# Two-layer attention on one core: eight ScalarE copies make a row tile that one VectorE product made

## The chip, the core and the metric

The kernel runs on one core of a Trainium2 chip. The metric is the device time of one execution in microseconds. Three runs of the kernel before gave 4740.17, 4742.67 and 4742.81 us: median 4742.67. Engine names: PE is TensorE, PEld its weight loads, DVE is VectorE, ACT is ScalarE, POOL is GpSimd, SP is SyncE, which issues most of the DMAs.

## What is computed

The input is a batch of two images with 256 channels of 64 x 64 points, so N = 4096 positions each. Layer 0 is an attention with four heads of width 16 and a gate; the change doesn't touch it. Layer 1, cut to what matters:

```
qkv = einsum('oc,bchw->bohw', w_qkv, x) + b_qkv        # 768 rows
q, k, v = split(qkv.reshape(b, 4, 3*64, N), 3, axis=2)  # four heads, width 64
attn = softmax(einsum('bhdn,bhdm->bhnm', q, k) / 8)
out = einsum('bhnm,bhdm->bhnd', attn, v).reshape(b, c, h, w)
return einsum('oc,bchw->bohw', w_out, out) + b_out + x
```

Note the reshape: the result of a head is laid out as rows of positions with 64 values each, and these rows are then read as channels.

## The kernel before

Layer 0 fills the first 2100 us or so of the span; layer 1 the rest.

Layer 1 is cut into 32 **units**: image b (2), pair of heads g (2), block j of 512 query positions (8). A unit runs over NM = 32 **chunks** of 128 key positions. The chunks form NG = 2 **groups** of GS = 16: each group has its own running maximum, its own sum of exponentials and its own accumulated output, and the two are joined at the end of the unit.

What one chunk costs, with the lines:

- `score` (L861): PE forms the scores of two heads into a PSUM pair of banks, 128 keys x 2 x 512 queries. The pool of pairs has two buffers.
- `keep` (L878, L879): DVE takes the running maximum; ACT copies the scores to SBUF, into a ring of 24 tiles called `raw`.
- `shift` (L944): some 20 chunks later DVE adds the negated maximum.
- `weigh` (L956, L968): ACT takes the exponential in place, POOL adds the tile to the group's sum `acc`. The first add of a group (L966) takes two tiles.
- `gather` (L978): PE multiplies by the values and accumulates `av` in PSUM.

So two streams run together: scores of the present chunk, and shift, exponential and gather of the chunk 20 places before.

At the end of a group: PE transposes the running maximum (`turn_max`, L886), DVE reduces it (`fold`, L898), POOL splits the result into three bf16 parts (`split`, L909 to L912), PE turns these back (`turn`, L925), ACT copies them (L930), PE spreads them (`spread_shift`, L939), and the next shift can start.

At the end of a unit, while the next unit's scores run: PE sums `acc` over the partitions (`total`), ACT copies the sums (L1016) and takes an exponential of 128x8 (L1018), PE transposes them, DVE forms the factors `f` (L1035 to L1038), POOL one more of them (L1039). Then, for the second group and after it for the first, PE transposes the accumulated output (`turn_sums`, L1023, through `turned`), and `rows` multiplies the turned tile by its factors: a 128 x 4 x 2 x 64 tile, where each of the 4 x 2 pieces of 64 has its own factor on every partition (L1049). For the second group POOL adds the bias (L1056), for the first POOL adds the two halves (L1060), and two DMAs on SP write the result out.

All these small PSUM results (the turned tiles, the turned maxima, the products for the queries, keys and values) use one pool with **one** bank, called misc. A product into it can start only when the previous user has been read.

The order on each engine is written out by hand: every instruction is kept in program order, and a table of hooks says in which step and at which place of it ("start", "early", "early end", "late", "late end") an extra piece stands. A step handles a pair of chunks. The hooks for the end of a unit are:

```
at(t1 + 5, "late", lambda u=u: turn_sums(u, 1))
at(t1 + 5, "late end", lambda u=u: rows(u, 1))
at(t1 + 6, "early", lambda u=u: turn_sums(u, 0))
at(t1 + 6, "early end", lambda u=u: rows(u, 0))
```

with `t1 = t0 + US + GS // 2`. Around them stand the score products of the next unit's chunks 28 to 31, and the product for the queries of the unit after it (`next_queries`, L672), which also uses misc and is copied by ACT (`keep_queries`, L699).

Of the kernel before, what the change touches and what calls it, by code (L numbers as in the profile page):

```python
# [10 lines left out]
AF = mybir.ActivationFunctionType  # L11
ALU = mybir.AluOpType
# [3 lines left out]
P = 128  # L16
# [5 lines left out]
D1 = 64  # L22
# [5 lines left out]
def conv_attention_kernel(  # L28
# [19 lines left out]
    nc = tc.nc  # L48
# [3 lines left out]
    PB = NB // P  # L52
# [167 lines left out]
    seq = tc.keep_in_program_order  # L220
# [24 lines left out]
    with own0:  # L245
# [134 lines left out]
        def prep_dyn(four):  # L380

            ps = prep_bank("dynp_{}_{}".format(*four[0]))
            for i, u in enumerate(four):
                seq(nc.tensor.matmul(
                    ps[32 * i : 32 * i + 32, :], c2rep, work.pop(("d1", *u)),
                    start=True, stop=True,
                ))
            rows = prep.tile([P, NB], F32, tag="dyn", bufs=1, name="dynrows_{}_{}".format(*four[0]))
            seq(nc.scalar.activation(rows, ps, AF.Identity, bias=c2b))
            for i, (b, j) in enumerate(four):  # L390
                nc.sync.dma_start(out=dyn0[b][j], in_=rows[32 * i : 32 * i + 1, :])
# [330 lines left out]
        for i in range(NJ):  # L722
            k = (0, 0, i)
# [54 lines left out]
    with (  # L778
# [10 lines left out]
        avs1, srows, losts, joined, halves = {}, {}, {}, {}, {}  # L789
# [255 lines left out]
        def rows(u, n):  # L1045
            b, g, j = u
            ps = avs1.pop((u, n))
            r = l1.tile([P, PB, 2, D1], F32, tag="rows", name=f"rows_{b}_{g}_{j}_{n}")
            seq(nc.vector.tensor_tensor(  # L1049
                r, ps, joined[u][:, n].unsqueeze(3).to_broadcast([P, PB, 2, D1]), ALU.mult  # L1050
            ))
            last = u == units[-1]
            if n == 1:
                halves[u] = r
                bias = b1v[:, 2 * g : 2 * g + 2, :].unsqueeze(1).to_broadcast([P, PB, 2, D1])
                seq(nc.gpsimd.tensor_tensor(r, r, bias, ALU.add))  # L1056
                return
            joined.pop(u)
            engine = nc.vector if last else nc.gpsimd
            seq(engine.tensor_tensor(r, r, halves.pop(u), ALU.add))  # L1060


            if last:
                for k in range(2):
                    c = ((2 * g + k) * N + j * NB) // D1 % P
                    for i in range(PB):
                        (nc.sync if k else nc.scalar).dma_start(
                            out=last_att[0][c + 2 * i : c + 2 * i + 2, :].rearrange(
                                "q (s d) -> q s d", d=D1
                            ),  # L1070
                            in_=r[:, i, k, :],
                        )
                return
            to = att[b].rearrange("(h q) (s d) -> h (q s) d", h=H, d=D1)
            for k in range(2):
                nc.sync.dma_start(
                    out=to[2 * g + k, bass.ts(j, NB), :].rearrange("(i q) d -> q i d", q=P),
                    in_=r[:, :, k, :],
                )
# [29 lines left out]
        for n, u in enumerate(units):  # L1109
# [32 lines left out]
            at(t1 + 5, "early end", lambda u=u: factors(u))  # L1142
# [4 lines that stand above are left out]
            if b < B - 1 and (g, j) == (PR - 1, NJ - 1):  # L1147
                for i in range(NJ):
# [156 lines left out]
```

## Time and profile before

| quantity | value |
|---|---|
| median of three runs | 4742.67 us |
| the profiled execution, its own time | 4741.58 us |
| its span in the profile | 4739.8 us |
| granted TensorE clock | 0.996 |
| L1049 on DVE | 64 instructions, median 686 ns |
| period of an ordinary unit of layer 1 | 81.30 us |
| period of four units that also project the first image out | 88.75 us |
| period of units that prepare no keys and values | 79.19 us |

The period is the distance between the starts of the first L1049 of neighbouring units. A line of the timeline has the start and the length in us, the engine, the line of the code, the operation, output and inputs with their shapes, the number of instructions merged into it, and in brackets the idle time of the engine just before it, with what ended that. In a line of the groups the three fields after the shapes are the busy time in us with the mean in ns, and the idle time before.

### The profile page before, as it was taken

Reading aid. Unit: us, or ns where it says so; the run is one execution under the profiler, and the core shown is the slowest. Engines: PE = TensorE matmul, PEld = TensorE weight load, DVE = VectorE, ACT = ScalarE, POOL = GpSimd, SP = SyncE. Lnnn points to the kernel's source line nnn. Section 1 sums busy time; section 2 is a strip of 40 time slices with the busy share of each in tenths; the row PEclk is TensorE's granted clock in tenths of the full one; section 3 lists DMA queues with packets and bytes.
Section 4 is the critical chain, followed back from the end, with each engine's and each line's share of the span. In section 5 each row is a group of like instructions: output and inputs, shape, how many; then the busy total and the mean of one; then the engine's idle time right before and its main releaser. Section 6 shows DMA issues by size and latency. Waiting matters only on the chain.

```text
span 4739.8 us, 70643 instructions
## 1 busy us (share of the span) xinstructions
PE 4526.9 (96%) x27506; PEld 1496.2 (32%) x27506; DVE 3917.0 (83%) x4584; ACT 3394.1 (72%) x4508; POOL 2540.6 (54%) x1491
## 2 busy tenths in 40 slices
PE   8999999999999999989999999999999999999998
PEld 3433333333333333333232232323233332222222
DVE  6777777777777777359999999999999899999996
ACT  3366666666666666668888888888887778888884
POOL 6300000000000000039999999999998889999994
PEclk9999999999999999999999999999999999999999
DMA  3100000000000000110000100001111111000002
GB/s 103 34 4 19 19 21 15 15 15 15 15 15 15 15 13 13 57 63 25 23 25 17 54 30 23 25 23 36 52 36 45 63 52 47 18 14 7 14 16 74
DMA packets 113381, 140.10 MB, mean 30 GB/s; under 512 B 51864, under 2 KB 52696, under 8 KB 112932
## 3 DMA queue, kind: packets, MB, share of 16 engines
q1 hardware_dynamic: 111260, 135.11, 9.2%
q8 instruction: 216, 3.54, 0.3%
q14 instruction: 121, 0.99, 0.1%
q10 hardware_dynamic: 1784, 0.46, 0.0%
HBM read 93.58 MB, written 41.70 MB: 29 GB/s over the span
## 4 chain that ended last, share of the span: by engine, by line
PE 58%; DVE 15%; POOL 15%; issue 6%; ACT 5%; DMA 1%; SPq 0%; ACTq 0%; DVEq 0%; POOLq 0%
PE s L448 24%; POOL acc L968 13%; PE av L463 12%; DVE rmax L878 10%; PE s L861 6%; PE av L978 5%; DVE raw L944 4%; ACT raw L879 4%; PE a L410 2%; PE p L270 1%; PE k1p L672 1%; POOL acc L966 1%; PE rt L886 1%; PE q1p L672 1%; PE o L549 1%
## 5 line engine op out<-in xcount | busy, mean ns | idle before, releaser
L968 POOL TENSOR_TENSOR acc<-acc,raw 128x1024 f32<-128x1024 f32 x884 | 2098.1, 2373 | 89.4 <-ACT raw L956 30.2
L414 DVE TENSOR_REDUCE mx<-a 128x1 f32<-128x512 f32 x2048 | 1315.3, 686 | 450.5 <-PE a L410 449.4
L451 ACT ACTIVATE p<-s 128x512 f32<-128x512 f32 x2048 | 1109.8, 597 | 701.3 <-PE a L410 367.3
L944 DVE TENSOR_TENSOR raw<-raw,shift 128x1024 f32<-128x1024 f32 x1024 | 1238.0, 1213 | 19.2 <-PE shift L939 12.7
L861 PE MATMUL s<-q,k 64*128 64x512 f32 x4096 | 1117.2, 636 | 142.9 <-ACT raw L879 134.6
L878 DVE TENSOR_TENSOR rmax<-s,rmax 128x1024 f32<-128x1024 f32 x960 | 1170.1, 1219 | 72.7 <-PE s L861 70.8
L879 ACT COPY raw<-s 128x1024 f32<-128x1024 f32 x1024 | 1037.7, 1013 | 259.4 <-DVE rmax L878 173.5
L448 PE MATMUL s<-q,kT 32*128 32x512 f32 x4096 | 1219.1, 640 | 0.0
L956 ACT ACTIVATE raw<-raw 128x1024 f32<-128x1024 f32 x1024 | 1086.9, 1062 | 178.4 <-DVE raw L944 147.3
L410 PE MATMUL a<-kT,q 32*128 32x512 f32 x4096 | 1129.7, 643 | 1.2 <-DVE mx L414 1.0
L978 PE MATMUL av<-raw,v 128*64 128x512 f32 x4096 | 999.3, 606 | 2.0
L463 PE MATMUL av<-p,v 128*32 128x256 f32 (+1 forms) x7904 | 650.2, 399 | 0.6 <-ACT avs L477 0.6
L861 PEld LDWEIGHTS s<-q,k 64*128 64x128 f32 x4096 | 317.1, 185 | 827.9 <-ACT raw L879 628.0
L513 POOL TENSOR_TENSOR f<-f,dyn 128x16 f32<-128x16 f32 x15 | 3.3, 223 | 1028.2 <-DVE f L512 1028.2
L448 PEld LDWEIGHTS s<-q,kT 32*128 32x128 f32 x4096 | 397.9, 183 | 426.3 <-issue 392.1
L978 PEld LDWEIGHTS av<-raw,v 128*64 128x64 f32 x4096 | 243.3, 136 | 587.6 <-issue 428.8
L463 PEld LDWEIGHTS av<-p,v 128*32 128x32 f32 x7904 | 157.6, 108 | 751.5 <-issue 737.3
L564 POOL TENSOR_SCALAR res<-res 128x1024 f32<-128x1024 f32 x16 | 16.8, 1049 | 660.5 <-ACT res L563 660.5
L410 PEld LDWEIGHTS a<-kT,q 32*128 32x128 f32 x4096 | 305.0, 184 | 31.4 <-DVE mx L414 18.2
L966 POOL TENSOR_TENSOR acc<-raw,raw 128x1024 f32<-128x1024 f32 x64 | 152.4, 2381 | 112.7 <-ACT raw L956 103.8
L898 DVE TENSOR_REDUCE negs<-rt 128x4 f32<-128x512 f32 x128 | 88.3, 690 | 50.1 <-PE rt L886 47.6
L318 DVE RECIPROCAL std<-std 128x128 f32<-128x128 f32 x64 | 56.1, 920 | 37.7 <-ACT std L313 37.7
(332 smaller groups left out, 1840.4 us busy)
## 6 DMA issues: line engine op xcount, KB each, us to landing
x<-in_x_dram SPq DMA_DIRECT2D x16, 512.0 KB
res<-in_x_dram SPq DMA_DIRECT2D x16, 512.0 KB
x<-res SPq DMA_DIRECT2D x16, 512.0 KB
att<-rows SPq DMA_DIRECT2D x62, 128.0 KB
kd<-k1s SPq DMA_DIRECT2D x24, 256.0 KB
vd<-v1s SPq DMA_DIRECT2D x24, 256.0 KB
k<-kd SPq DMA_DIRECT2D x24, 256.0 KB
v<-vd SPq DMA_DIRECT2D x24, 256.0 KB
```

Source lines behind the costliest of these rows:

```text
L410: seq(nc.tensor.matmul(ps, qs0[u][r, bass.ts(i, P)], kTs[b][r, bass.ts(m, NB)], start=True, stop=True,))
L414: seq(nc.vector.tensor_reduce(mxs[u][:, i * H + h, m : m + 1], ps, AX.X, ALU.max))
L448: seq(nc.tensor.matmul(ps, kTs[b][r, bass.ts(m, P)], qs0[u][r, :], start=True, stop=True))
L451: seq(nc.scalar.activation(pt[:, k, :], ps, AF.Exp, scale=D0**-0.5))
L463: seq(nc.tensor.matmul(avs[u][32 * h : 32 * h + 32, cols], vs0[b][:, m, 32 * h : 32 * h + 32], pts[t, h // 2][:, h % 2, cols], start=(m == ...
L861: seq(nc.tensor.matmul(ps[:, k, :], ks[b, g, m // PB][r, bass.ts(m % PB, P)], qs1[u][r, :], start=True, stop=True,))
L878: seq(nc.vector.tensor_tensor(rmax[u, n], ps, before, ALU.max))
L879: seq(nc.scalar.copy(raw, ps))
L944: seq(nc.vector.tensor_tensor(raws[t], raws[t], shifts[u, t % NM // GS], ALU.add))
L956: seq(nc.scalar.activation(p, p, AF.Exp, scale=D1**-0.5))
L968: seq(nc.gpsimd.tensor_tensor(accs[u, n], accs[u, n], p, ALU.add))
L978: seq(nc.tensor.matmul(avs1[u, n][k * D1 : (k + 1) * D1, :], v[:, m % PB, k, :], raws[t][:, k, :], start=(m % GS == 0), stop=(m % GS == GS ...
```

## The change

In `rows`, the tile of the second group (n == 1) is made on ScalarE by eight activations, one for each of the 4 x 2 pieces of 64 columns, with the function Copy and the factor as a scale per partition. The tile of the first group stays on VectorE, and so do both tiles of the last unit. The rest is as before: POOL adds the bias to the same tile.

```
             r = l1.tile([P, PB, 2, D1], F32, tag="rows", name=f"rows_{b}_{g}_{j}_{n}")
-            seq(nc.vector.tensor_tensor(
-                r, ps, joined[u][:, n].unsqueeze(3).to_broadcast([P, PB, 2, D1]), ALU.mult
-            ))
             last = u == units[-1]
+            if n == 1 and not last:
+                for i in range(PB):
+                    for k in range(2):
+                        seq(nc.scalar.activation(
+                            r[:, i, k, :], ps[:, i, k, :], AF.Copy,
+                            scale=joined[u][:, n, i, k : k + 1],
+                        ))
+            else:
+                seq(nc.vector.tensor_tensor(
+                    r, ps, joined[u][:, n].unsqueeze(3).to_broadcast([P, PB, 2, D1]), ALU.mult
+                ))
             if n == 1:
```

## The prediction

> **What bounds the kernel now.** I read the engine shares first, then a table of busy time over one unit of layer 1, then the timeline around the changed step, and last the groups for the durations of ScalarE's instructions.
>
> The engine shares say only that no engine can be left out:
> ```profile
> PE 4526.9 (96%) x27506; PEld 1496.2 (32%) x27506; DVE 3917.0 (83%) x4584; ACT 3394.1 (72%) x4508; POOL 2540.6 (54%) x1491
> ```
> In layer 1 the units repeat with a fixed period. One period of it (columns: window, length, then busy time of PE, PEld, DVE, ACT, POOL):
> ```profile
> core 0: us, PE busy (x) PEld busy (x) DVE busy (x) ACT busy (x) POOL busy (x), PEclk, DMA share, GB/s
> 3167.52:3248.82 81.30, 76.69 (x330) 24.33 (x330) 76.35 (x72) 68.51 (x73) 75.52 (x43) 1.00 0.08 23
> ```
> PE 94%, DVE 94%, POOL 93%, ACT 84%: three engines share the bound, so what counts is which wait ends last where the change sits. The start of the first L1049 (call it t) in two units, and the bias add that follows it on POOL:
> ```profile
> 3004.79 0.69 DVE L1049 TENSOR_TENSOR rows<-turned,f 128x512 f32<-128x512 f32 x1
> 3007.45 1.28 POOL L1056 TENSOR_TENSOR rows<-rows,b1v 128x512 f32<-128x512 f32 x1
> 3086.23 0.69 DVE L1049 TENSOR_TENSOR rows<-turned,f 128x512 f32<-128x512 f32 x1 [0.16 <-PE turned L1023]
> 3088.74 1.28 POOL L1056 TENSOR_TENSOR rows<-rows,b1v 128x512 f32<-128x512 f32 x1
> ```
> One period is 81.30 us nearly everywhere (88.75 in the four units that also project the first image out, 79.19 in those that prepare no keys). In the second unit here L1049 comes 0.14 us late (81.44 later) while POOL is on time (81.29 later); the unit after it (t = 3167.52, its L1056 at 3170.18 below) is late by that 0.14 in both. So a delay in this stretch lasts, and POOL doesn't absorb it. Now the stretch itself, at t = 3167.52:
> ```profile
> 3167.41 2.40 PE L861 MATMUL s<-q,k 64*128 64x512 f32 x8
> 3167.52 0.69 DVE L1049 TENSOR_TENSOR rows<-turned,f 128x512 f32<-128x512 f32 x1
> 3167.61 1.01 ACT L879 COPY raw<-s 128x1024 f32<-128x1024 f32 x1 [0.62 <-POOL acc L968]
> 3168.13 1.21 DVE L944 TENSOR_TENSOR raw<-raw,shift 128x1024 f32<-128x1024 f32 x1
> 3169.38 1.06 ACT L956 ACTIVATE raw<-raw 128x1024 f32<-128x1024 f32 x1 [0.75 <-DVE raw L944]
> 3169.74 0.66 PE L1023 MATMUL turned<-ident,avs 128*128 128x128 f32 x4
> 3170.18 1.28 POOL L1056 TENSOR_TENSOR rows<-rows,b1v 128x512 f32<-128x512 f32 x1
> 3170.33 1.94 PE L978 MATMUL av<-raw,v 128*64 128x512 f32 x8
> 3171.52 0.68 DVE L1049 TENSOR_TENSOR rows<-turned,f 128x512 f32<-128x512 f32 x1
> 3172.26 1.12 PE L672 MATMUL q1p<-b_('q', (0, 1, 6))_25737,w 128*128 128x512 f32 x2
> 3174.51 0.30 PEld L861 LDWEIGHTS s<-q,k 64*128 64x128 f32 x4 [0.90 <-ACT raw L879]
> ...
> 3188.26 0.40 PE L925 MATMUL nm1p<-ident,negmax 128*128 128x128 bf16 x4 [0.54 <-POOL negmax L912]
> ...
> 3190.05 1.13 PE L861 MATMUL s<-q,k 64*128 64x512 f32 x4 [0.33 <-ACT raw L879]
> ```
> What to see: PE goes from scores to the second turn (3169.74), gather, and query product without a gap; the second turn starts as the scores end. The turned tile is PSUM's one "misc" bank, so the second turn also needs the first to have been read: today that is done at 3168.21, 1.5 us early. PE's path and DVE's (rows, shift, max, shift, rows to 3172.20) meet at the query product within about 0.06 us. Both are critical; ACT idles 0.75 us in between.
>
> [...]
> ```profile
> L995 ACT COPY avs<-av 128x512 f32<-128x512 f32 x49 | 29.1, 593 | 0.0
> L699 ACT ACTIVATE q<-q1p,b 128x512 f32<-128x512 f32 x25 | 16.8, 672 | 0.0
> L1018 ACT ACTIVATE lost<-lost 128x8 f32<-128x8 f32 x25 | 5.3, 213 | 0.0
> ```
> A pointer adds 672 - 593 = 79 ns, and the start of the next instruction lies about 100 ns before the end in all three. [...] the built instruction list of the changed kernel has the same three table loads as before, so no switch is charged.
>
> **The change, part by part.**
>
> Removed: 31 of the 64 L1049 on DVE (the last unit keeps its own). Each occupies DVE for 0.61 us (3167.52 to 3168.13), 18.9 us in all. It only counts where DVE alone is late.
>
> Added: 31 x 8 = 248 activations of 128x64 from PSUM. From the 1024- and 512-element copies the slope is (1013 - 593) / 512 = 0.82 ns per element, so one lasts 672 - 448 x 0.82 = 305 ns, and one starts every 205 ns. 8 x 0.205 = 1.64 us of ACT per unit, 51 us in all. Bounds: 150 ns (the 110 ns of L1018's start to start plus 46 for 56 more elements, the pointer free) and 300 ns (no overlap).
>
> Order, read off the built list: the eight stand on ACT behind the copy L879 at t + 0.09 and ahead of the exponential L956. No DMA, SP or GpSimd instruction changes place. Only the first waits (for PE's turn, long done). They start at t + 1.00 (the next instruction follows 0.91 after a 1024-element copy) and end at t + 1.00 + 7 x 0.205 + 0.305 = t + 2.74.
>
> Behind them on ACT: the exponential starts at t + 2.64 instead of t + 1.86, ends at 3.70, and the gather that reads it is due on PE at about 4.3, so 0.6 us of slack hides it. The score copies after it: the first is 0.4 us later, with its bank not wanted until t + 5.8; the next comes earlier than now, as DVE is ahead. Cost zero; if the eight took over 300 ns each, this cover would go.
>
> Who waits for the eight: (a) POOL's bias add, at t + 2.66 now, would start at 2.80: 0.14 late. POOL's next stall is on its own input, and PE's wait for POOL at 3188.26 is followed by a 0.33 us wait for ACT at 3190.05, so 0.33 us of this costs nothing. (b) PE's second turn, at t + 2.22 now, must wait for the bank: 2.74 + 0.06 (the gap from an ACT end to the PE start it releases, 3168.62 to 3168.68) = t + 2.80. PE stalls 0.58 us, with everything queued behind in order: gather, query product, scores, the max transposes.
>
> What PE gets back: 0.06 at the query product, and 0.11 at the score at 3174.51 (3173.32 to the next product at 3175.57 is 2.25 us for what elsewhere takes 2.14, waiting for a copy behind DVE, which is now earlier). Net 0.58 - 0.17 = 0.41 us per unit. From there to the second max transpose PE has no gap, and DVE's next reduce waits for it, so it lasts to the next unit.
>
> Sum: 26 ordinary units x 0.41 = 10.7 us. In the four long units the query product waits 0.40 us for DVE's second rows today, and PE's stall of about 0.5 takes its place: 0.05 each, 0.2 in all. In the last of the 31 no query product follows and DVE is the late one: 0.5 back. Total 10.4 us. The profiled execution took 4741.58 us (span 4739.80 and 1.78 around it), 1.09 below the median of 4742.67: 4752.0 against its own time, 4753 against the median.
>
> **The rivals.**
>
> 1. Not slower: POOL's chain sets the period, and PE's slip vanishes in its 0.54 us wait for the split at 3188.26. Then only POOL's 0.14 us stays, 31 x 0.14 = 4.3 us: 4747. Or the eight are quicker than I think: at one per 170 ns they cost 0.13 a unit, 4747. For it: POOL is 93% busy and that wait is real. Against: the unit at 3086.23, whose 0.14 us passed a punctual POOL. It decides if the slip stays below 0.54 and the wait at 3190.05 were not there.
> 2. Much slower: no overlap, or a pointer reload per copy. At one per 250 to 300 ns the slip is 0.77 to 1.07 us a unit instead of 0.41: 31 times that is 24 to 33 us, 4767 to 4776. No row shows eight small pointer activations in a row, so this stays open; L699 among its neighbours speaks against.
> 3. Faster: DVE alone is the bound, and 31 x 0.61 = 18.9 us come back: 4724. The point is the bank: the eight would have to end before t + 2.16, so one per 130 ns, and even then PE's path allows only 0.17 us a unit (4737). DVE's 94% speaks for it, the seamless PE against.
> 4. That the change isn't done as said is excluded by the built list (248 activations in place, 31 DVE rows gone).
>
> **How the numbers follow.** A measurement here tells about 0.2%, 9.5 us, from no change: the limits are 4733 and 4752.2. My forecast, 4749 to 4760, has 0.55, of which 0.45 lies above 4752.2; rival 1 (4742 to 4749) 0.22; rival 2 (from 4760 up) 0.19; rival 3 0.04. Slower 0.45 + 0.19 = 0.64, same 0.10 + 0.22 = 0.32, faster 0.04. The range from 4744 to 4772 leaves out rival 3, the lowest of rival 1 and the upper half of rival 2.
>
> **What would show it.** In the changed profile: the eight at 300 ns each, one every 205; PE idle about 0.58 us before the second turn, released by ACT; DVE's second rows at about t + 3.5 with a wait for PE; the period 81.7 us. Wrong if the period stays at 81.30 with that stall there (rival 1), if the eight take over 2 us together (rival 2), or if the second turn doesn't wait (rival 3).

## The result and the profile after

The changed kernel takes 4755.47 us (median of eight runs, 4754.04 to 4756.58). The kernel before, run beside it, takes 4741.19 (4740.17 to 4742.81). The ratio is 1.0029, 95% interval 1.0018 to 1.004: slower by 0.29%, with an interval from 0.18 to 0.4%. That is 2.5 us above the predicted 4753.0, which was reckoned from the median of 4742.67; set against the kernel before as it ran beside, 14.3 us were added where 10.4 had been forecast. The profiled execution took 4755.49 us, its span is 4753.7 (4739.8 before), the granted clock 0.996 as before: the difference to explain is 13.9 us of span.

Line numbers move with the change: in the profile after, L1053 are the eight activations, L1058 is VectorE's row (L1049 before) and L1064 is POOL's bias add (L1056 before).

The engine shares of the page after, first; they moved as the instruction counts say and do not show a loss:
```profile
PE 4519.8 (95%) x27506; PEld 1498.6 (32%) x27506; DVE 3900.1 (82%) x4553; ACT 3428.2 (72%) x4756; POOL 2538.7 (53%) x1491
```
The table of one ordinary unit shows it (window, length, then the busy time of each engine):
```profile
core 0: us, PE busy (x) PEld busy (x) DVE busy (x) ACT busy (x) POOL busy (x), PEclk, DMA share, GB/s
3174.51:3256.32 81.81, 76.43 (x330) 24.41 (x328) 75.80 (x72) 69.67 (x83) 75.42 (x43) 1.00 0.08 23
```
The period, here from one unit's first L1053 to the next one's, went from 81.30 to 81.81 us. DVE has 0.55 us less to do in it and ACT 1.16 more, and every engine but ACT idles more than before: PE 5.38 us of the unit instead of 4.61. So the added 0.51 us is a wait on PE and not work of PE's.

The timeline of the changed stretch. It answers to the stretch shown of before, and its times are to be set against that one's plus 5.99 us, by which the unit stands later up to here (first L879 of both lists):
```profile
3173.60 1.01 ACT L879 COPY raw<-s 128x1024 f32<-128x1024 f32 x1 [0.62 <-POOL acc L968]
3174.51 1.75 ACT L1053 ACTIVATE rows<-turned,f 128x64 f32<-128x64 f32 x8
3176.09 1.12 ACT L956 ACTIVATE raw<-raw 128x1024 f32<-128x1024 f32 x1
3176.31 0.66 PE L1023 MATMUL turned<-ident,avs 128*128 128x128 f32 x4 [0.52 <-ACT rows L1053]
3176.34 1.28 POOL L1064 TENSOR_TENSOR rows<-rows,b1v 128x512 f32<-128x512 f32 x1 [0.17 <-ACT rows L1053]
3177.06 0.69 DVE L1058 TENSOR_TENSOR rows<-turned,f 128x512 f32<-128x512 f32 x1
3178.77 1.13 PE L672 MATMUL q1p<-b_('q', (0, 1, 6))_25821,w 128*128 128x512 f32 x2
3179.82 1.99 PE L861 MATMUL s<-q,k 64*128 64x512 f32 x8
3181.00 1.23 DVE L878 TENSOR_TENSOR rmax<-s,rmax 128x1024 f32<-128x1024 f32 x1 [0.99 <-PE s L861]
3181.74 1.12 PE L672 MATMUL q1p<-b_('q', (0, 1, 6))_25821,w 128*128 128x512 f32 x2
3185.07 2.03 PE L861 MATMUL s<-q,k 64*128 64x512 f32 x8 [0.34 <-ACT q L699]
3190.18 0.69 DVE L898 TENSOR_REDUCE negs<-rt 128x4 f32<-128x512 f32 x1 [0.64 <-PE rt L886]
3194.39 0.40 PE L925 MATMUL nm1p<-ident,negmax 128*128 128x128 bf16 x4 [0.16 <-POOL negmax L912]
3196.55 1.13 PE L861 MATMUL s<-q,k 64*128 64x512 f32 x4 [0.71 <-ACT raw L879]
```
and the lines of before that are needed beside it and were not shown yet:
```profile
3175.57 1.12 PE L672 MATMUL q1p<-b_('q', (0, 1, 6))_25737,w 128*128 128x512 f32 x2
3178.57 2.03 PE L861 MATMUL s<-q,k 64*128 64x512 f32 x8
3180.53 0.66 PE L886 MATMUL rt<-ident,rmax 128*128 128x128 f32 x4
3183.68 0.69 DVE L898 TENSOR_REDUCE negs<-rt 128x4 f32<-128x512 f32 x1 [0.63 <-PE rt L886]
```
Following the slip, each line's time less its time before and less 5.99: the second turn 0.58 (its own idle time is 0.52), the first half of the query product 0.52, its second half 0.18, the next group of scores 0.51 with a wait of 0.34 for ACT's query copy L699, DVE's reduce 0.51, the shift transpose nm1p only 0.14, the scores after it 0.51. So PE nearly catches up twice (at 3181.74 and at 3194.39) and both times a wait for ACT puts it back.

The view of line L1053, the added instructions: fastest, median and slowest in ns, then who waited for them (us in all, times):
```profile
L1053 ACT ACTIVATE rows<-turned,f x248: 316/336/368, 2192.8 to 4660.3; 128x64 f32<-128x64 f32 x124
  PE turned L1023: 15.9, 31
  POOL rows L1064: 2.8, 7
```
PE waits for them in each of the 31 units, 15.9 us in all: already more than the 13.9 us lost.

### The profile page after: what moved, and what is told of

The parts are those of the page before. It is cut to its first block, busy times and chain, and to the rows that moved or that the text cites. A ratio compares the mean times of both kernels' runs of the same rounds, so it can differ in the third digit from the quotient of the medians.

```text
span 4753.7 us, 70860 instructions
## 1 busy us (share of the span) xinstructions
PE 4519.8 (95%) x27506; PEld 1498.6 (32%) x27506; DVE 3900.1 (82%) x4553; ACT 3428.2 (72%) x4756; POOL 2538.7 (53%) x1491
## 4 chain that ended last, share of the span: by engine, by line
PE 58%; POOL 15%; DVE 13%; ACT 7%; issue 6%; DMA 1%; SPq 0%; ACTq 0%; DVEq 0%; POOLq 0%
PE s L448 24%; POOL acc L968 13%; PE av L463 12%; DVE rmax L878 9%; PE s L861 6%; PE av L978 5%; DVE raw L944 4%; ACT raw L879 3%; ACT raw L956 2%; PE a L410 2%; POOL acc L966 1%; PE p L270 1%; ACT rows L1053 1%; PE rt L886 1%; PE k1p L672 1%
## 5 line engine op out<-in xcount | busy, mean ns | idle before, releaser
L878 DVE TENSOR_TENSOR rmax<-s,rmax 128x1024 f32<-128x1024 f32 x960 | 1169.2, 1218 | 102.9 <-PE s L861 101.7
L879 ACT COPY raw<-s 128x1024 f32<-128x1024 f32 x1024 | 1037.9, 1014 | 262.6 <-DVE rmax L878 175.5
L898 DVE TENSOR_REDUCE negs<-rt 128x4 f32<-128x512 f32 x128 | 88.2, 689 | 50.0 <-PE rt L886 47.5
```

The source lines that it names most:

```text
L878: seq(nc.vector.tensor_tensor(rmax[u, n], ps, before, ALU.max))
L879: seq(nc.scalar.copy(raw, ps))
```

## The experiments

**The theory.** The loss comes from how long the turned tile's one PSUM bank is held: a reader that starts 1.0 us later on ACT and takes 1.75 us keeps PE from its second turn, and the slip travels with the scores. **Rivals.** A: ACT's queue has 1.6 us more in it per unit, and what stands behind (exponential, score copies) comes late, whatever bank it reads. B: DVE is the bound, and only the size of the relief matters. C: POOL's late bias add sets the period.

### Half on each engine

Edit on the changed kernel: VectorE takes the first two of the four blocks in one instruction, ScalarE the other two in four.
```
-                for i in range(PB):
+                seq(nc.vector.tensor_tensor(
+                    r[:, :2], ps[:, :2],
+                    joined[u][:, n, :2].unsqueeze(3).to_broadcast([P, 2, 2, D1]), ALU.mult
+                ))
+                for i in range(2, PB):
```


> VectorE makes the pieces of the first two query blocks of the second group's tile in one instruction, ScalarE the other four pieces. Theory (the bank is held): ScalarE's four end about 1.95 us after the mark t (the time at which the turned tile is ready for the first reader), before the second turn is due at t + 2.22, so TensorE doesn't stall and the time goes back to that of the kernel before: 4739 to 4743 us. Rival A (it is ScalarE's added work in its queue): half of the work leaves half of the loss, about 4748. Rival B (VectorE's work is what bounds the unit): 31 x 0.27 us are gained, about 4733.

Measured: 4738.39 us (4736.67 to 4739.16) beside 4740.99 of the kernel before; ratio 0.9994 (0.9986 to 1.0002). The period is 81.20 us. Its timeline, one unit earlier than in the lists above, as are the later ones with times near 3100 (L1051 is VectorE's half, L1057 ScalarE's four):
```profile
3084.33 0.42 DVE L1051 TENSOR_TENSOR rows<-turned,f 128x256 f32<-128x256 f32 x1
3085.33 0.94 ACT L1057 ACTIVATE rows<-turned,f 128x64 f32<-128x64 f32 x4
3086.54 0.66 PE L1023 MATMUL turned<-ident,avs 128*128 128x128 f32 x4
3095.30 2.03 PE L861 MATMUL s<-q,k 64*128 64x512 f32 x8 [0.19 <-ACT q L699]
```
The four are done at 3086.27, the second turn starts 0.27 us later without a wait, and the whole loss is gone. Half of ACT's added load is still there, so A would have kept about half the loss. The period is 0.10 us shorter than before for 0.27 us less on VectorE, so relief of DVE seems worth something, but less than its size (the interval of the ratio includes 1): B doesn't bound alone.

### ScalarE's load without the bank

Edit on the kernel before: seven activations of the same form at the same place, reading and writing SBUF tiles that nobody waits for.
```
             last = u == units[-1]
+            if n == 1 and not last:
+                spare = l1.tile([P, 7, D1], F32, tag="spare", bufs=1, name=f"spare_{b}_{g}_{j}")
+                for i in range(7):
+                    seq(nc.scalar.activation(
+                        spare[:, i, :], b1v[:, 0, :], AF.Copy,
+                        scale=joined[u][:, n, i // 2, i % 2 : i % 2 + 1],
+                    ))
```


> The kernel before, with seven extra activations of 128x64 on ScalarE at the place where the changed kernel has its eight. They read a constant in SBUF and write a spare tile that nobody reads, so they add work that the result doesn't need. [...] Theory (the bank is held): VectorE still frees the bank early, TensorE's second turn doesn't wait, and the time stays within 3 us of the kernel before: 4741 to 4745. Rival A (ScalarE's added work): the whole loss appears, about 4755.

Measured: 4741.26 us; ratio 1.0001 (0.9993 to 1.0009), period 81.33. Its timeline:
```profile
3167.17 0.69 DVE L1049 TENSOR_TENSOR rows<-turned,f 128x512 f32<-128x512 f32 x1
3168.17 1.79 ACT L1056 ACTIVATE spare<-b1v,f 128x64 f32<-128x64 f32 x7
3169.38 0.66 PE L1023 MATMUL turned<-ident,avs 128*128 128x128 f32 x4
3169.86 1.04 ACT L956 ACTIVATE raw<-raw 128x1024 f32<-128x1024 f32 x1
```
The seven start one per 0.24 us where the eight start one per 0.20, so ACT is occupied for 1.79 us, as long as by the eight, and the exponential comes after them; PE's turn doesn't wait, and nothing is lost. What reaches PE is that the next gather lasts 2.06 us instead of 1.94, and the unit absorbs it. A is out for this place: the same load costs nothing when the bank is left to VectorE.

### The bank held late, without the load

Edit on the kernel before: VectorE makes the tile as before, and one more ScalarE copy of 64 columns of the same bank stands just ahead of the second turn. Its output is unused.
```
+                held[u] = ps
...
+        def peek(u):
+            spare = l1.tile([P, D1], F32, tag="spare", bufs=1, name="spare_{}_{}_{}".format(*u))
+            seq(nc.scalar.copy(spare, held.pop(u)[:, 0, 0, :]))
...
+            if u != units[-1]:
+                at(t1 + 6, "early", lambda u=u: peek(u))
             at(t1 + 6, "early", lambda u=u: turn_sums(u, 0))
```


> The kernel before, with one extra ScalarE copy of 128x64 from the turned tile of the second group, placed behind the exponential that follows; what it writes is not used. It adds only about 0.2 us of ScalarE work per unit but holds the bank until about t + 3.1. Theory (the bank is held): the second turn on TensorE starts at t + 3.15 instead of t + 2.22, 0.06 of that is given back, 0.88 us a unit remain: 31 x 0.88 = 27 us, about 4768. Rival A (ScalarE's added work): an eighth of the loss, about 4743. Rival B (VectorE's relief counts): no change, 4741.

Measured: 4765.04 us; ratio 1.0051 (1.0037 to 1.0065), period 82.06. Its timeline:
```profile
3176.79 0.69 DVE L1049 TENSOR_TENSOR rows<-turned,f 128x512 f32<-128x512 f32 x1
3178.64 1.06 ACT L956 ACTIVATE raw<-raw 128x1024 f32<-128x1024 f32 x1 [0.76 <-DVE raw L944]
3179.42 1.30 POOL L1058 TENSOR_TENSOR rows<-rows,b1v 128x512 f32<-128x512 f32 x1
3179.60 0.19 ACT L1085 COPY spare<-turned 128x64 f32<-128x64 f32 x1
3179.85 0.33 PE L1023 MATMUL turned<-ident,avs 128*128 128x128 f32 x1 [0.78 <-ACT spare L1085]
```
One copy of 190 ns per unit, on an engine that had just idled 0.76 us ahead of its exponential, costs 24.05 us, or 0.76 a unit: what PE waits for the bank, and not what the instruction lasts. POOL's bias add starts 2.63 us after VectorE's row, as in the kernel before (2.66), so it is not late here and C isn't needed for the loss. Together with the run before, this carries the theory from both sides: load without the hold is free, and the hold without the load costs.

### The query copy ahead of the score copy

In the changed kernel PE had recovered to a slip of 0.18 by its second half of the query product, and lost it again by waiting for ACT's query copy. That copy stands on ACT behind a score copy and an exponential that wait for DVE, and DVE's maximum (L878 at 3181.00) had itself waited 0.99 us for the late scores: the slip goes round PE's recovery by way of DVE and ACT. Edit on the changed kernel: a new hook ahead of the exponential's step, and the query copy moved to it.
```
-                at(t0 - 1, "early end", lambda u=u: keep_queries(u))
+                at(t0 - 1, "before weigh", lambda u=u: keep_queries(u))
...
+                hung(t, "before weigh")
```


> The changed kernel, with the copy of the next queries on ScalarE moved ahead of one exponential. In the changed kernel TensorE makes up 0.33 us at the last scores of a unit and loses it again waiting for this copy. Theory (the copy is where the given-back time is lost): the copy ends about 0.95 us earlier, that wait of 0.34 us goes, 26 to 31 units x 0.33 = 9 to 10 us return: about 4746. Rival (the loss is passed on another way, by the chain of maxima and the transposes): no change, 4755.

Measured: 4748.27 us; ratio to the kernel before 1.0015 (1.0008 to 1.0021), so some 7 us of the loss are gone, less than the 9 to 10 expected. The period is 81.63.
```profile
3173.41 0.66 PE L1023 MATMUL turned<-ident,avs 128*128 128x128 f32 x4 [0.52 <-ACT rows L1053]
3179.40 1.01 ACT L879 COPY raw<-s 128x1024 f32<-128x1024 f32 x1 [1.21 <-DVE rmax L878]
3180.31 0.69 ACT L699 ACTIVATE q<-q1p,b 128x512 f32<-128x512 f32 x1
3181.76 2.28 PE L861 MATMUL s<-q,k 64*128 64x512 f32 x8
```
The stall at the turn stays at 0.52, and the wait for the query copy is gone. But the group of scores now lasts 2.28 us instead of 2.03: ACT's score copy ends only inside it, at 3182.85 (1.01 us from 3181.84), and its second half probably waits for that. Of the 0.33 us that PE could have kept, 0.18 a unit is kept.

### Half and half with the moved copy, and the moved copy alone

The first run has both edits; the second has the moved query copy on the kernel before.

> The half-and-half kernel (VectorE makes four pieces of the second group's tile in one instruction, ScalarE the other four), with the copy of the next queries on ScalarE moved ahead of one exponential. In the half-and-half kernel TensorE still waits 0.19 us a unit for that copy, and behind it 0.61 us for GpSimd's split, of which 0.26 is covered by a later wait. Theory (that copy is now what ends last): 26 to 31 units x 0.19 are gained over 4738.4: about 4733. Rival (GpSimd's split sets the unit now): no gain, 4738.

> The kernel before, with only the copy of the next queries on ScalarE moved ahead of one exponential. Theory (in the kernel before VectorE's path holds up the last scores of a unit, so the copy isn't late there): no change, 4739 to 4742. Rival (the copy is late in every version): the gain of 7 us that it brought in the changed kernel comes here too, 4734.

Measured: half and half with the moved copy 4734.53 us (4732.96 to 4735.8), ratio 0.9985 (0.9979 to 0.9992), period 81.06: faster than the kernel before by 0.15%. The moved copy alone 4738.12, ratio 0.9992 (0.9984 to 1.0), period 81.18. The interval of the second reaches 1, but the period of its trace is 0.12 us shorter. So the copy was tied for last in the kernel before as well, which I had not expected: moving it gains 0.12 a unit there, 0.14 on top of the half, 0.18 in the changed kernel. The kernel before, first two lines, and the moved copy alone:
```profile
3176.63 1.94 PE L978 MATMUL av<-raw,v 128*64 128x512 f32 x8
3178.56 0.30 PEld L861 LDWEIGHTS s<-q,k 64*128 64x128 f32 x4 [0.88 <-ACT q L699]
3175.41 1.94 PE L978 MATMUL av<-raw,v 128*64 128x512 f32 x8
3177.28 1.99 PE L861 MATMUL s<-q,k 64*128 64x512 f32 x8
```
From the gather to the scores it takes 1.94 us before (3176.63 to 3178.57) and 1.87 with the moved copy. The list gives PE no idle time in the first; the starts show it, and so does the weight load's wait. The scores then take 1.96 us to the next transpose (3178.57 to 3180.53) and 1.91 with the moved copy, which is the rest of the 0.12. The timeline of half and half with the moved copy:
```profile
3085.78 0.66 PE L1023 MATMUL turned<-ident,avs 128*128 128x128 f32 x4
3094.27 2.14 PE L861 MATMUL s<-q,k 64*128 64x512 f32 x8
```
From the turn to these scores it takes 8.49 us, with no wait in the list between them, where half and half alone takes 8.76 and the changed kernel 8.76 behind its stall.

### The query product elsewhere, and the turn later

If PE alone sets this stretch, then work taken out of it should give its length back, up to the next other limit. Edit on the kernel before: the query product (two halves, 2.1 us of PE) moved four and five steps earlier, with its fetch and its copy.
```
-                at(t0 - 5, "start", lambda u=u, b=b, j=j: fetch(("q", u), x1[b][j]))
-                at(t0 - 2, "late", lambda u=u: next_queries(u, 0))
-                at(t0 - 1, "early", lambda u=u: next_queries(u, 1))
-                at(t0 - 1, "early end", lambda u=u: keep_queries(u))
+                at(t0 - 9, "start", lambda u=u, b=b, j=j: fetch(("q", u), x1[b][j]))
+                at(t0 - 6, "late", lambda u=u: next_queries(u, 0))
+                at(t0 - 6, "late", lambda u=u: next_queries(u, 1))
+                at(t0 - 6, "late end", lambda u=u: keep_queries(u))
```


> The kernel before, with the product for the next queries and its copy moved five steps ahead, out of the stretch in which TensorE has no gap, to the middle of the unit. Theory (that stretch sets the unit): up to 1.0 us a unit leaves the stretch, but GpSimd's split allows only 0.33 of it: about 10 us gained, 4731. Rival (TensorE is as full in the middle of the unit): the 2.1 us come back there, 4741 or above.

The second run makes this edit on the changed kernel and also turns the first group's sums later, behind the gather (`turn_sums(u, 0)` at `(t1 + 6, "late")`, `rows(u, 0)` at `(t1 + 6, "late end")`), so that the eight have time to end.

> The changed kernel, with the query product five steps ahead and, on TensorE, the second turn behind the two gathers that follow it, so that the eight activations have freed the bank when it is due. Theory (the bank is held): TensorE's stall of 0.5 us is gone although ScalarE still makes all eight, and the time is within 4 us of the kernel with only the early query product. Rival A (ScalarE's added work): some 14 us above that kernel.

Both missed. The first took 4764.1 us, ratio 1.0046 (1.0033 to 1.0058), period 82.22, where I had expected a gain. The first two lines are from the product's new place, the others from its old one:
```profile
3079.26 1.98 PE L672 MATMUL q1p<-b_('q', (0, 1, 5))_25130,w 128*128 128x512 f32 x4
3086.99 1.13 PE L861 MATMUL s<-q,k 64*128 64x512 f32 x4 [0.91 <-ACT raw L879]
3098.28 0.66 PE L1023 MATMUL turned<-ident,avs 128*128 128x128 f32 x4
3100.66 1.22 DVE L878 TENSOR_TENSOR rmax<-s,rmax 128x1024 f32<-128x1024 f32 x1
3101.99 1.01 ACT L879 COPY raw<-s 128x1024 f32<-128x1024 f32 x1 [0.75 <-PE s L861]
3103.05 1.13 PE L861 MATMUL s<-q,k 64*128 64x512 f32 x4 [1.19 <-ACT raw L879]
3108.61 0.66 PE L886 MATMUL rt<-ident,rmax 128*128 128x128 f32 x4
```
At the old place the second half of the scores starts 4.77 us after the turn (3098.28 to 3103.05), and in the kernel before, with half of the product still ahead of it, it starts 4.77 us after it too (3169.74 to 3174.51). What sets it in both is the line of DVE's row, DVE's maximum and ACT's score copy; the profile names PE for the copy's wait here, but in program order the copy follows the maximum that ends at 3101.88, and in the kernel before the same copy waits 0.75 us for DVE by name. So PE waits 1.19 us there, and from the turn to the first max transpose only 0.46 us of the 2.1 come back (10.33 us against 10.79). The unit is 0.92 longer all the same, so the new place costs 1.38: the product takes 1.98 us there in one piece, of which an idle time of PE right behind it takes up a part (0.72 in the kernel before, at 3153.95), and a wait for ACT further on is 0.91 where it was 0.45 (3158.45). Why that wait grew was not tried apart.

The second took 4776.25, ratio 1.0072 (1.0059 to 1.0086), period 82.62, 0.40 above the first where I had expected the two to agree:
```profile
3101.60 1.75 ACT L1053 ACTIVATE rows<-turned,f 128x64 f32<-128x64 f32 x8
3104.35 1.08 PE L978 MATMUL av<-raw,v 128*64 128x512 f32 x4 [0.46 <-ACT raw L956]
3105.36 0.65 PE L1023 MATMUL turned<-ident,avs 128*128 128x128 f32 x4
3106.11 0.69 DVE L1058 TENSOR_TENSOR rows<-turned,f 128x512 f32<-128x512 f32 x1 [0.95 <-issue]
3112.48 1.13 PE L861 MATMUL s<-q,k 64*128 64x512 f32 x4 [1.13 <-ACT raw L879]
```
The bank's wait is gone, as intended. In its place the gather, now ahead of the turn, waits 0.46 us for the exponential behind the eight. The 0.6 us of slack that hid the late exponential came from the turn and PE's stall, which both stood ahead of the gather. The turn is later for both reasons, its new place and that wait; DVE's row starts as the turn ends, after 0.95 us of idling, and DVE then has no gap up to the maximum whose score copy PE waits for (1.13 us at 3112.48). So rival A has a point from which it matters: once the gather comes first, ACT's queue is one link of the chain that ends last. How much of the 0.40 is the queue's and how much the later turn's was not tried apart.

## Why the prediction was right, and what was off

**Right: the mechanism and its place.** PE's second turn waits for the eight, in each of the 31 units. The slip of its start is 0.58 in the unit shown, as predicted, and the eight end 2.75 us after the mark t, which is 3173.51 here (2.74 predicted).

**The eight copies.** They last 336 ns at the median and not 305, but start one per 0.20 us against 0.205 (1.75 us from the first start to the last end, less the last one's length, by seven). The prediction took both from the slope of the large copies and the overlap in the trace before; the length was 31 ns short, and the rate, which matters, was right. The profile after shows three table loads of 1.28 us, as the one before does, so the eight added none. Rival 2's rate of 250 to 300 is out. Two of the rivals' sums count eight intervals where only seven lie between the starts: one per 250 ns would make the slip 0.73 and not 0.77, one per 170 ns 0.17 and not 0.13.

**The step that was off: what PE gets back.** I took 0.06 at the query product and 0.11 at the score that waited for a copy behind DVE, 0.17 in all. The first came as said (0.58 to 0.52). The second was larger than thought (0.52 to 0.18): I had set the 2.25 us of that group of scores against 2.14 elsewhere, but 2.14 holds a wait too, and a group without one takes 1.92 (after, 3179.82 to 3181.74). Then almost all of it was lost at the next scores, where PE waits 0.34 for the query copy, a wait that I had put at nothing. What is kept is 0.07, so the slip is 0.51 instead of 0.41. My statement that PE has no gap from there to the second max transpose held only for the idle times that the list gives: by the starts PE already waited 0.07 for that copy in the kernel before, and the moved copy gained 0.12 a unit there. I had looked for slack on PE alone and not on the line that feeds it. That the total came out within 2.5 us of the forecast is therefore in part luck: one give-back was taken too small and its loss was left out.

**How the slip gets past POOL.** Rival 1 was half true: at nm1p PE stands only 0.14 late, since POOL's split sets it, and the wait for POOL fell from 0.54 to 0.16. But the wait for ACT's score copy right after it grew from 0.33 to 0.71, by the same 0.38. The slip doesn't go over PE there but over DVE, as the prediction had it: the reduce L898 waits for PE's max transposes, is 0.51 late, and the score copies follow DVE. POOL's own delay was 0.17 against 0.14, and cost nothing.

**The sum.** The distances between neighbouring units (reciprocal to reciprocal on DVE) add up as follows:

| distances | predicted | measured |
|---|---|---|
| 24 ordinary | 24 x 0.41 = 9.8 | 11.75 (0.51 in nearly all) |
| 5 around the long units | 4 x 0.05 + 0.41 = 0.6 | 1.09 |
| the one before the last | 0.41 | 0.86 |
| the last | -0.5 | -0.42 |
| before the first unit and after the last | 0 | 0.62 |
| all | 10.4 | 13.9 |

Of the 3.5 us that were missing, the give-back explains 1.9 in the ordinary units: 24 x 0.10, less about 0.4 by which three of before's distances were irregular (81.43, 79.30, 79.46). The rest is 0.5 around the long units, 0.5 in the last two and 0.6 outside; these were not tried apart.

**B, the relief of DVE**, is what let PE recover from 0.58 to 0.18: with the extra copy and no relief the turn was 0.84 late (t + 3.06) and only 0.08 came back. But in the changed kernel no more than 0.07 of the recovery was kept. How busy DVE is doesn't settle what its relief is worth: it was busy for 94% of a unit before, and moving all of the row lost 0.29% while moving half of it gave a ratio of 0.9994 (0.9986 to 1.0002), no certain gain, and 0.9985 (0.9979 to 0.9992) with the query copy moved as well.

## What to carry to other kernels

When a reader of a single PSUM buffer moves to another engine, price first the time at which the buffer is given back and who waits for it, and only then the engine time: here 1.8 us of ScalarE cost nothing and a 0.19 us read at the wrong moment cost 24 us. If the idle engine is slower or starts later, split the read between the two engines so that both end before the next writer is due: here ScalarE's half ended 0.27 us ahead of the second turn, and the loss was gone. An engine that runs without a gap in the trace may be tied with others, as PE was here with ACT's query copy (0.12 us a unit); look at what each of its next inputs waits for before you count on it catching up.

## What was not expected

- The query copy was tied for last in the kernel before, though PE's lines showed no idle time there: the order of two ScalarE instructions was worth 0.12 us a unit, 3.7 us in 31 units and near what was measured (ratio 0.9992).
- 2.1 us of PE work per unit, moved from a stretch where PE's lines showed no idle time to one where PE had gaps, made each unit 0.92 us longer: 0.46 came back at the old place, where DVE's line was tied with PE, and the new place cost 1.38.
